# VectorE's list work in a four-layer graph network: list 0 spread over layer 0, one order chain in products 2 and 3, row gathers ahead of pair gathers

## The chip, the cores and the metric

The kernel runs on one core of a Trainium2 chip. The metric is the device time of one execution in microseconds (us), the median of several runs. The core has five engines that work from queues of their own: TensorE (PE in the profile, with its weight loads as PEld), VectorE (DVE), ScalarE (ACT), GpSimd (POOL) and SyncE (SP, which here only issues loads). They wait for each other through semaphores.

## What is computed

Four graph layers over the same 4096 x 4096 adjacency matrix `adj` (float32, about 1 entry in 500 not zero, a full diagonal), with `x` of 4096 x 128:

```python
x = _layernorm(x + _L0_gnn_ref(x, adj, adj, L0_gnn_W, L0_gnn_a))   # attention over positive entries
x = _layernorm(x + _L1_gnn_ref(x, adj, ...))                       # two Chebyshev convolutions, K = 3
x = _layernorm(x + _L2_gnn_ref(x, adj, ...))                       # attention with 4 heads
x = _layernorm(x + _L3_gnn_ref(x, adj, ...))                       # (adj @ h / deg) W_neigh + h W_self

# in layer 1
def cheb_conv(x, L, W, b):
    Tx0 = x
    out = Tx0 @ W[0]
    Tx1 = L @ x
    out = out + Tx1 @ W[1]
    for k in range(2, W.shape[0]):
        Tx2 = 2.0 * (L @ Tx1) - Tx0
        out = out + Tx2 @ W[k]
        Tx0, Tx1 = (Tx1, Tx2)
    return out + b
```

So layer 1 needs four products with `adj`: product 1 (`adj @ x`), product 2 (`adj @ t1`), product 3 and a fourth one (the code runs that one inside the function for the sparse layers).

## The kernel before

**Chunks and blocks.** `adj` is stored transposed and cut into 8 x 8 chunks of 512 x 512. A load brings one chunk of 1 MB as a tile [128, 4, 512]; five buffers (`ld`) take turns, and every load is issued on SP's queue. A block `ib` is a column of eight chunks. In products 1 to 3 one chunk means eight TensorE instructions of line 714 (4 matmuls in float32, each of two passes) into the block's sum `pacc`. `propagate` runs over blocks and chunks, and after each chunk it calls a hook `seen(ib, n, c, a)`. The hooks of a product are numbered through: h = 0 to 47 in product 2 (blocks 2 to 7, eight chunks each), h = 0 to 39 in product 3 (blocks 3 to 7). A dictionary `plan` says what is begun at which hook.

**Lists.** Since `adj` is sparse, the kernel also makes a list of the entries of each row. `take` finds, for each of the four rows of 128 in a chunk, the eight largest entries and their places (`max`, line 1359, and `max_index`, line 1360). A diagonal chunk is first copied by ScalarE, quarter by quarter, into the one buffer `copied` (line 1356), and VectorE takes the diagonal out (line 1358). `build(c)` turns what was found for group c of rows into a list, in three steps: step 1 sorts (and gives `count`, line 1386), then TensorE multiplies it (line 1410), step 2 makes `spread`, TensorE multiplies again (line 1434), and step 3 gives the indices that the gathers use. Groups 0, 1 and 2 (`PAIRED`) are finished early. List 0 is found in layer 0 by `first_list`, four rows in one go whenever a chunk with j = 0 comes by (lines 377 and 378).

**Gathers.** With lists 0 and 1 the blocks 0 and 1 of product 2 are left out of the dense product: their 8 units of 128 rows are summed from gathered rows. `pull(u)` issues nine indirect loads on GpSimd (line 1480), each followed by a small `pause` (line 1526); `weigh(u)` multiplies and adds the rows on VectorE (lines 1514 and 1517); `product(u)` gives them to TensorE (lines 1587 and 1589). In product 3 blocks 0, 1 and 2 are done so (12 units, lines 1645 to 1656), each `product(u)` calling `pull(u + 2)`; in the fourth product, blocks 0 and 1 again (lines 1989 and 1991). `fetch(c, n)` issues n of the 36 gathers of `pairs` for group c (the entries that a row has in both directions), and `paired(c)` puts them in place; a unit of group c can only be weighed behind that. `values(c)` issues 12 gathers of entries for group c.

**Block ends.** In product 2 VectorE makes `t2T` out of `pacc` (line 762), and `second_end` gives it to TensorE (lines 769 and 774) with ScalarE and VectorE between (lines 701 to 704). In product 3 ScalarE copies `pacc` (line 805), TensorE transposes, VectorE copies the result (line 807), and the rows are stored in a table in HBM from which later gathers read.

**Order.** Outside of the last layers the instructions of an engine are put in order by a planner, at build time, from costs and due times that it reckons with. `tc.keep_in_program_order` pins an instruction to the order of the program. In product 2 the takes, the adds of `weigh` (line 1517) and `paired` are pinned so, and on GpSimd every gather; steps of `build`, the block ends' `t2_of` and the copies of line 807 are the planner's to place.

**Layer 0** reads each chunk once, in two passes over rows i: VectorE makes a mask `pos` of the chunk (line 329), TensorE sums it (line 398), ScalarE counts bad entries (line 382), and TensorE multiplies the chunk (line 410). When a row of eight chunks is done, `scores(i)` copies the sums (`parts`, line 445), and TensorE goes on from there (line 405). `keep_busy` adds idle matmuls (line 341) in the first rows.

Of the kernel before, what the change touches and what calls it, by code (L numbers as in the profile page):

```python
# [11 lines left out]
F32 = mybir.dt.float32  # L12
# [34 lines left out]
def adj_resnorm_d4(ctx: ExitStack, tc: tile.TileContext, x_in, xT_in, adj, adjT, pairs, diag_in, w0g, w0gT, a0, w1a, b1a,  # L47
# [234 lines left out]
    def layer0(ld, ps_acc, ps_tr, ps_mm):  # L282
# [9 lines left out]
        with tc.tile_pool(name="l0", bufs=1) as l0, tc.tile_pool(name="l0w", bufs=2) as l0w, \  # L292
# [74 lines left out]

            def first_list(i, a):
                top, at = firsts
                for k in range(TB):  # L370
                    row = a[:, k, :]
                    if i == 0:
                        row = x[:, k * TB:(k + 1) * TB, :].rearrange("p t f -> p (t f)")
                        nc.scalar.copy(row, a[:, k, :])
                        d = row[:, k * P:(k + 1) * P]
                        nc.vector.scalar_tensor_tensor(d, ident, less_own[0][:, k:k + 1], d, op0=ALU.mult, op1=ALU.add)
                    nc.vector.max(top[:, k, i, :], row)
                    nc.vector.max_index(at[:, k, i, :], top[:, k, i, :], row)

# [79 lines left out]
            for i in range(2):  # L459
# [5 lines left out]
                for n, j in enumerate(order):  # L465
# [14 lines left out]
                    if j == 0:  # L480
                        first_list(i, a)
                    if n == 1 and rest:
                        diagonal_product(*rest)
                        diagonal_sums(*rest)
# [15 lines left out]
            def sums_of(i, j, pe, first, last, pool=ld, name="chunk"):  # L500
# [4 lines left out]
                if j == 0:  # L505
                    first_list(i, a)
                return j, a, pos
# [5 lines left out]
            for i in range(2, NB):  # L513
# [55 lines left out]
                if i == 5:  # L569
                    tc.keep_in_program_order(nc.sync.dma_start(x, x_in.rearrange("(t p) f -> p t f", p=P)))  # L570
# [91 lines left out]
    degrees, firsts, less_own = [], [], []  # L662

    def network(usual):

        with ExitStack() as whole:
# [3 lines left out]
            with ExitStack() as first, ExitStack() as l1h_pool:  # L670
                ps_acc, ps_tr, ps_mm = [first.enter_context(tc.tile_pool(name=n, bufs=2, space=PSUM, reuse_waits="tile"))
                                        for n in ("ps_acc", "ps_tr", "ps_mm")]
                if usual:
# [4 lines left out]
                    less_own[:] = [early.tile([P, NT], F32, name="less_own")]  # L678
                    nc.scalar.dma_start(own_entries, diag_in)
                    nc.vector.tensor_scalar_mul(less_own[0], own_entries, -1.0)  # L680
# [10 lines left out]
                l1w = l1h_pool.enter_context(tc.tile_pool(name="l1w", bufs=2, reuse_waits="tile"))  # L691
                l1h = l1h_pool.enter_context(tc.tile_pool(name="l1h", bufs=1, reuse_waits="tile"))
# [5 lines left out]
                def elu(dst, p, bias, less):  # L698
                    r = l1w.tile([P, IB], F32, name="elu_r", bufs=1)
# [61 lines left out]
                def t2_of(t2T, p, cols):  # L761
                    nc.vector.scalar_tensor_tensor(t2T, p, 2.0, xT[:, cols], op0=ALU.mult, op1=ALU.subtract)
# [20 lines left out]
                for ib, blk, p in propagate(lambda jt: t1[:, jt, :], seen=second, blocks=[b for b in range(NB) if not usual or b not in LAST]):  # L783
                    t2T = l1w.tile([P, IB], F32, name="t2T")
                    t2_of(t2T, p, blk)
# [17 lines left out]
                for ib, blk, p in propagate(lambda jt: v[:, jt, :], beside=times_w1, seen=third, blocks=[b for b in range(NB) if not usual or b not in PAIRED]):  # L803
# [3 lines left out]
                    nc.vector.tensor_copy(w[:, ib * TB:(ib + 1) * TB, :], q)  # L807
                    if usual:
                        lists.store(1, ib, w)
# [480 lines left out]

    class Lists:
# [3 lines left out]
        def __init__(self, whole, first, layer, own_entries):  # L1295
# [9 lines left out]
            self.diag = own_entries  # L1305
            self.source = keep.tile([P, NT, NEAR + QT], I32, name="source")
# [41 lines left out]

        def take(self, ib, c, a, pinned=False):
            pin = tc.keep_in_program_order if pinned else lambda r: r  # L1350
            for k in range(TB):
                t = c * TB + k
                row = a[:, k, :]
                if ib == c:
                    row = self.keep.tile([P, IB], F32, name="copied")
                    nc.scalar.copy(row, a[:, k, :])
                    d = row[:, k * P:(k + 1) * P]
                    pin(nc.vector.scalar_tensor_tensor(d, ident, less_own[0][:, t:t + 1], d, op0=ALU.mult, op1=ALU.add))
# [3 lines left out]
        def indices(self, out, key):  # L1362

            miss = self.work.tile([P, key.shape[1], key.shape[2]], F32, name=f"miss{key.shape[2]}", bufs=1)
            nc.vector.tensor_scalar(miss, key, 0.0, float(N + 1), op0=ALU.is_le, op1=ALU.mult)
            nc.vector.scalar_tensor_tensor(out, key, -1.0, miss, op0=ALU.add, op1=ALU.add)

        def build(self, c, pinned=False):
            pin = tc.keep_in_program_order if pinned else lambda r: r
            work = self.work  # L1370
# [11 lines left out]
            nc.vector.tensor_scalar(flat(there), flat(top), 0.0, None, op0=ALU.is_gt)  # L1382
            nc.vector.tensor_reduce(deg, rows(there), AX.X, ALU.add)
            nc.vector.tensor_reduce(self.bad[:, 2, c:c + 1], deg, AX.X, ALU.max)
            nc.vector.tensor_scalar(deg, deg, float(-NEAR), 0.0, op0=ALU.add, op1=ALU.max)
            nc.vector.tensor_copy(count, deg)
            nc.vector.tensor_copy(flat(key), flat(found_at))
            nc.vector.tensor_tensor(rows(key), rows(key), self.first.rearrange("p s r -> p (s r)")[:, None, :].to_broadcast([P, TB, NB * 8]), ALU.add)
            nc.vector.tensor_mul(flat(key), flat(key), flat(there))
            pairs = top.rearrange("p k s r -> p (k s) r")  # L1390
            nc.vector.tensor_reduce(self.bad[:, 0, c:c + 1], pairs[:, :, 7], AX.X, ALU.max)
            nc.vector.tensor_tensor(twice, pairs[:, :, 0:7], pairs[:, :, 1:8], ALU.is_equal)
            nc.vector.tensor_mul(twice, twice, pairs[:, :, 1:8])
            nc.vector.tensor_reduce(self.bad[:, 1, c:c + 1], twice, AX.XY, ALU.max)
            for k in range(TB):
                row, left = rows(key)[:, k], rows(there)[:, k]
                for n in range(0, MOST, 8):
                    nc.vector.max(best[:, k, n:n + 8], row if n == 0 else left)
                    if n + 8 < MOST:
                        nc.vector.match_replace(left, best[:, k, n:n + 8], row if n == 0 else left, -1.0)  # L1400
# [719 lines left out]
```

## Time and profile before

| | us |
|---|---|
| median of 3 runs | 1672.21 (1670.91 to 1673.08) |
| the profiled execution | 1672.15 |
| its span, first to last instruction | 1670.4 |
| layer 0 | about 0 to 351 |
| product 1 | about 351 to 577 |
| product 2 | 577 to 834 |
| product 3 | 834 to 1037 |
| fourth product | 1037 to 1235 |
| gathered layers 2 and 3 | 1235 to 1670 |

| engine | busy in the span | in product 2 | in product 3 |
|---|---|---|---|
| TensorE | 89% | 233 of 257 us | 186 of 203 us |
| VectorE | 66% | 194 us | 121 us |
| GpSimd | 50% | 176 us | 160 us |
| ScalarE | 22% | 44 us | 15 us |

The stages are cut where TensorE's instructions go from one line to the next. A row of the timeline gives the start, the duration, the engine, the line, the operation, out<-in by the program's names, the shapes and the count; in square brackets stands the idle time of the engine just before, and what ended it. Where several instructions of one kind follow each other they are one row.

### The profile page before, as it was taken

To read this page: it belongs to the slowest core of one execution; us is meant where nothing else is said; L and a number is where in the kernel's file an instruction comes from. 1 tells how busy PE (TensorE), PEld (TensorE's weight loads), DVE (VectorE), ACT (ScalarE), POOL (GpSimd) and SP (SyncE) were. 2 spreads that over 40 slices of the span, in tenths; PEclk is the share of its full clock that TensorE was granted. 3 is DMA by queue.
4 is the path that set the end of the run, shared out by engine and by line. 5 is a ranking of instruction groups with operands and counts; after the bars stand their busy time and mean duration, and the time that the engine had idled before them with its cause. 6 is when DMAs were issued, how large, how long until landed. Compare 5 with 4: busy or idle time off the path is not lost.

```text
span 1670.4 us, 16412 instructions
## 1 busy us (share of the span) xinstructions
PE 1480.9 (89%) x4744; PEld 719.1 (43%) x4744; DVE 1096.5 (66%) x3204; ACT 374.8 (22%) x690; POOL 835.3 (50%) x1322
## 2 busy tenths in 40 slices
PE   5799999999999999599979899999945788888886
PEld 3344344554444444244434444454423344444444
DVE  4887554788979696977669622255435766656676
ACT  5575450110000011112200000022223111122234
POOL 0000000000234048848768878888727888888851
PEclk9899999999999999799989899999976788889998
DMA  9776775578798977476568878988846667778773
GB/s 346 301 292 252 277 251 209 193 250 307 286 345 307 310 267 265 144 262 218 197 236 287 277 252 284 328 297 286 294 106 186 196 205 239 243 239 264 250 190 104
DMA packets 106972, 419.30 MB, mean 251 GB/s; under 512 B 21556, under 2 KB 44088, under 8 KB 67064
## 3 DMA queue, kind: packets, MB, share of 16 engines
q1 hardware_dynamic: 59984, 360.01, 60.4%
q0 software_dynamic: 22656, 36.17, 8.6%
q10 hardware_dynamic: 24232, 21.98, 4.4%
q8 instruction: 39, 0.64, 0.2%
q14 instruction: 61, 0.50, 0.1%
HBM read 404.39 MB, written 13.70 MB: 250 GB/s over the span
## 4 chain that ended last, share of the span: by engine, by line
PE 50%; DVE 20%; POOL 12%; DMA 9%; issue 6%; ACT 3%; SPq 1%; ACTq 0%; DVEq 0%; POOLq 0%
PE pacc L714 19%; PE pacc L410 11%; PE pp L2013 7%; POOL got L1783 5%; DMA got<-table,source 5%; DVE at L1360 3%; POOL got L1480 3%; DVE top L1359 2%; PE pp L1894 2%; POOL both_ways L1480 2%; DMA got<-rows,source 2%; POOL idle L1526 2%; DVE gw L1819 2%; DVE acc L1907 2%; DMA chunk<-in_adjT 1%
## 5 line engine op out<-in xcount | busy, mean ns | idle before, releaser
L1783 POOL DMA_INDIRECT got<-table,source x288 | 275.8, 958 | 88.3 <-issue 61.6
L1894 PE MATMUL pp<-chunk,xT 128*128 128x512 f32 x496 | 245.5, 637 | 1.0 <-ACT xT L1865 0.7
L714 PE MATMUL pacc<-chunk,x 128*128 128x512 f32 x512 | 222.6, 593 | 0.0
L1480 POOL DMA_INDIRECT got<-rows,source x180 | 181.4, 1008 | 56.6 <-issue 27.1
L410 PE MATMUL pacc<-chunk,hw 128*128 128x512 f32 x408 | 192.1, 616 | 0.2
L1328 POOL IOTA i<- 128x384 int32 (+3 forms) x4 | 0.9, 238 | 360.7 <-PE pden L398 345.0
L2013 PE MATMUL pp<-chunk,w 128*128 128x512 f32 x384 | 170.2, 592 | 0.0
L714 PE MATMUL pacc<-chunk,t 128*128 128x512 f32 x384 | 170.0, 593 | 0.0
L714 PEld LDWEIGHTS pacc<-chunk,x 128*128 128x128 f32 x512 | 96.0, 190 | 114.9 <-issue 114.9
L714 PE MATMUL pacc<-chunk,v 128*128 128x512 f32 x320 | 144.9, 604 | 0.0
L1480 POOL DMA_INDIRECT both_ways<-in_pairs,both_at x108 | 106.7, 988 | 72.7 <-DVE both_at L1462 55.5
L1359 DVE MAX8 top<-chunk 128x8 f32<-128x512 f32 x196 | 128.4, 677 | 17.6 <-DMA chunk<-in_adjT 17.6
L1894 PEld LDWEIGHTS pp<-chunk,xT 128*128 128x128 f32 x496 | 95.4, 205 | 91.6 <-issue 85.8
L1360 DVE FIND_INDEX8 at<-top,chunk 128x8 uint16<-128x512 f32 x196 | 133.0, 684 | 0.0
L410 PEld LDWEIGHTS pacc<-chunk,hw 128*128 128x128 f32 x408 | 76.6, 196 | 93.7 <-issue 90.1
L1526 POOL TENSOR_TENSOR idle<-idle 128x1 f32<-128x1 f32 x489 | 111.2, 227 | 8.5
L1517 DVE SCALAR_TENSOR_TENSOR here<-got,back,here 128x128 f32<-128x128 f32 x120 | 42.2, 351 | 100.9 <-DMA got<-rows,source 98.7
L714 PEld LDWEIGHTS pacc<-chunk,t 128*128 128x128 f32 x384 | 71.1, 190 | 81.0 <-issue 81.0
L329 DVE TENSOR_SCALAR pos<-chunk 128x2048 bf16<-128x2048 f32 x66 | 80.2, 1220 | 37.5 <-DMA chunk<-in_adjT 29.8
L382 ACT ACTIVATE junk<-chunk 128x2048 fp8e4<-128x2048 f32 x51 | 97.4, 1910 | 32.9 <-DMA chunk<-in_adjT 32.2
L2013 PEld LDWEIGHTS pp<-chunk,w 128*128 128x128 f32 x384 | 70.5, 190 | 76.5 <-issue 76.5
L714 PEld LDWEIGHTS pacc<-chunk,v 128*128 128x128 f32 x320 | 60.5, 194 | 78.2 <-issue 78.2
(381 smaller groups left out, 2021.1 us busy)
## 6 DMA issues: line engine op xcount, KB each, us to landing
chunk<-in_adjT SPq DMA_DIRECT2D x326, 1024.0 KB, 5.9
keep<-in_adjT SPq DMA_DIRECT2D x13, 1024.0 KB, 8.3
spread<-spread ACTq DMA_DIRECT2D x16, 384.0 KB, 3.5
got<-table,source POOLq DMA_INDIRECT x288
chunk<-in_adjT ACTq DMA_DIRECT2D x4, 1024.0 KB
got<-rows,source POOLq DMA_INDIRECT x180
table<-rows ACTq DMA_DIRECT2D x8, 264.0 KB, 6.7
xT<-in_xT ACTq DMA_DIRECT2D x8, 256.0 KB, 6.7
```

The lines of the kernel that those rows point to most:

```text
L329: r = nc.vector.tensor_scalar(pos, a, 0.0, None, op0=ALU.is_gt)
L382: nc.scalar.activation(junk, a, AF.Relu, scale=-1.0, accum_out=bad[:, n:n + 1], saturate=False)
L410: in_order(nc.tensor.matmul(p, hw[:, j * TB + k, :], a[:, k, :], start=first and k == 0, stop=last and k == TB - 1))
L714: nc.tensor.matmul(p, stationary(c * TB + k), a[:, k, :], start=n == 0 and k == 0, stop=n == NB - 1 and k == TB - 1)
L1359: pin(nc.vector.max(self.top[:, t, ib, :], row))
L1360: pin(nc.vector.max_index(self.at[:, t - TB, ib, :], self.top[:, t, ib, :], row))
L1480: tc.keep_in_program_order(nc.gpsimd.indirect_dma_start(out, None, of, bass.IndirectOffsetOnAxis(ap=index, axis=0)))
L1517: r = nc.vector.scalar_tensor_tensor(here, got[:, j, 0:F], self.back[:, u, j:j + 1], here, op0=ALU.mult, op1=ALU.add)
L1526: return nc.gpsimd.tensor_tensor(self.idle[:, 0:1], of, self.idle[:, 1:2], ALU.mult)
L1783: nc.gpsimd.indirect_dma_start(got[t][:, j, :], None, table, bass.IndirectOffsetOnAxis(ap=lists.source[:, t, j:j + 1], axis=0))
L1894: nc.tensor.matmul(p, y[:, t0 + k, :], a[:, ib % (TB // n), k, :], start=k == 0, stop=k == n - 1)
L2013: nc.tensor.matmul(p, w[:, c * TB + k, :], a[:, k, :], start=n == 0 and k == 0, stop=n == NB - 1 and k == TB - 1)
```

## The change

It has five parts.

1. **List 0 in layer 0.** `first_list` no longer works on the chunk: ScalarE copies the whole chunk into one half of the tile `x` (not in use yet), and the four row searches are put in a deque, one to be taken out after each of the following chunks. What is left is taken when the next chunk with j = 0 comes. The load of `x` moves from row i = 5 to row i = 7. The diagonal is set to zero with a comparison in place of an added negative, so the tile `less_own` goes, and the load of the diagonal moves from the program's start to the set-up of the lists.
2. **One chain in products 2 and 3.** `chained` gives each VectorE instruction of the takes, the list steps, `weigh` (now with the `hot` tiles, line 1514), `paired`, the block ends' `t2_of` and the copies of line 807 an order-only dependency on the one before it in the program. `product`'s own VectorE instructions and the block ends' line 704 are not in it.
3. **Order of chunks in product 2.** 0, 4, 1, 5, 2, 6, 3, 7 in place of 0 to 7. Only chunks with c of 4 or more have takes there.
4. **Hooks of product 2.** The rows of units 0 and 1 are pulled at hook 0, ahead of list 1's 36 pair gathers; list 2 is built from hook 14 on, in place of 8; the units are weighed at other hooks, units 0 and 1 early, and their space is used again for units 2 and 3.
5. **Product 3.** Three row buffers in place of two; no gathers of `values(3)` at hook 5, both `values` at hook 36; the units are weighed up to three hooks earlier.

The buffer `copied` moves to another pool, where it shares its place with `elu_r` of the block ends.

```diff
+            takes = deque()
+
             def first_list(i, a):
                 top, at = firsts
-                for k in range(TB):
-                    row = a[:, k, :]
+                rows = a
+                if i < NB - 1:
+                    while takes:
+                        takes.popleft()()
+                    rows = x[:, i % 2 * (NT // 2):(i % 2 + 1) * (NT // 2), :].rearrange("p (k t) f -> p k (t f)", k=TB)
+                    nc.scalar.copy(rows, a)
+
+                def take(k):
+                    row = rows[:, k, :]
                     if i == 0:
-                        row = x[:, k * TB:(k + 1) * TB, :].rearrange("p t f -> p (t f)")
-                        nc.scalar.copy(row, a[:, k, :])
                         d = row[:, k * P:(k + 1) * P]
-                        nc.vector.scalar_tensor_tensor(d, ident, less_own[0][:, k:k + 1], d, op0=ALU.mult, op1=ALU.add)
+                        nc.vector.scalar_tensor_tensor(d, ident, 0.0, d, op0=ALU.is_equal, op1=ALU.mult)
                     nc.vector.max(top[:, k, i, :], row)
                     nc.vector.max_index(at[:, k, i, :], top[:, k, i, :], row)
+
+                for k in range(TB):
+                    takes.append(lambda k=k: take(k))
+                if i == NB - 1:
+                    while takes:
+                        takes.popleft()()
...
                     if j == 0:
                         first_list(i, a)
+                    elif takes and i and n > 1:
+                        takes.popleft()()
...
-                if i == 5:
+                if i == 7:
                     tc.keep_in_program_order(nc.sync.dma_start(x, x_in.rearrange("(t p) f -> p t f", p=P)))
...
-                    less_own[:] = [early.tile([P, NT], F32, name="less_own")]
-                    nc.scalar.dma_start(own_entries, diag_in)
-                    nc.vector.tensor_scalar_mul(less_own[0], own_entries, -1.0)
...
-                for ib, blk, p in propagate(lambda jt: t1[:, jt, :], seen=second, blocks=[b for b in range(NB) if not usual or b not in LAST]):
+                for ib, blk, p in propagate(lambda jt: t1[:, jt, :], order=[0, 4, 1, 5, 2, 6, 3, 7], seen=second, blocks=[b for b in range(NB) if not usual or b not in LAST]):
                     t2T = l1w.tile([P, IB], F32, name="t2T")
-                    t2_of(t2T, p, blk)
+                    r = t2_of(t2T, p, blk)
+                    if usual:
+                        lists.chained(r)
...
-                    nc.vector.tensor_copy(w[:, ib * TB:(ib + 1) * TB, :], q)
+                    r = nc.vector.tensor_copy(w[:, ib * TB:(ib + 1) * TB, :], q)
                     if usual:
+                        lists.chained(r)
...
+        def chained(self, r):
+            if self.last is not None:
+                tc.add_manual_dep(r.ins, self.last.ins.name, mybir.DependencyInfo(
+                    mybir.DependencyClass.NoSync, mybir.DependencyReason.DATA), reason="chained")
+            self.last = r
+            return r
...
         def build(self, c, pinned=False):
             pin = tc.keep_in_program_order if pinned else lambda r: r
+            vector = in_order_engine(nc.vector, self.chained) if pinned else nc.vector
...
-        got = places[0:2] + places[2:4] * (units // 2 - 1)
+        got = places[0:2] * 2 + places[2:4] * 2
...
-        for c, h in ((1, 0), (2, 8)):
-            build = lists.build(c)
+        for c, h in ((1, 0), (2, 14)):
+            build = lists.build(c, True)
             for n in range(3):
                 at(h + 3 * n, next, build)
-        at(6, fetch, 1, TB * E)
-        at(11, pull, 0)
-        at(12, pull, 1)
-        at(17, fetch, 2, 9)
-        at(18, lists.paired, 0)
-        at(30, lists.paired, 1)
-        for u, h in enumerate((20, 24, 28, 32, 33, 37, 40, 41)):
+        at(0, pull, 0)
+        at(0, pull, 1)
+        at(7, fetch, 1, TB * E)
+        at(8, lists.paired, 0)
+        at(26, lists.paired, 1)
+        for u, h in enumerate((9, 11, 27, 30, 33, 35, 41, 44)):
             at(h, weigh, u)
             at(h + 1, product, u)
-        for u, h in ((2, 25), (3, 25), (4, 29), (5, 33), (6, 34), (7, 38)):
+        for u, h in ((2, 12), (3, 13), (4, 25), (5, 25), (6, 35), (7, 37)):
             at(h, pull, u)
-        at(40, fetch, 2, TB * E)
+        at(26, fetch, 2, 12)
+        at(45, fetch, 2, TB * E)
...
-                got[u] = pool.tile([P, E, F], F32, name="got3")
+                got[u] = pool.tile([P, E, F], F32, name="got3", bufs=3)
...
-        plan = {5: [lambda: deque(lists.values(3), 0)]}
-        for u, h in enumerate((7, 9, 15, 18, 20, 23, 25, 28, 31, 33, 36, 38)):
+        plan = {}
+        for u, h in enumerate((6, 9, 11, 14, 16, 19, 22, 24, 27, 30, 32, 35)):
...
-        plan[36].append(lambda: deque(lists.values(4), 0))
+        plan[36].append(lambda: (deque(lists.values(3), 0), deque(lists.values(4), 0)))
```

## The prediction, made before the changed kernel was run

> **What bounds the kernel now.** I read the table by stages first, since each stage has its own limit.
>
> ```profile
> core 0: us, PE busy (x) PEld busy (x) DVE busy (x) ACT busy (x) POOL busy (x), PEclk, DMA share, GB/s
> 354.00:577.00 223.00, 223.00 (x562) 100.07 (x562) 195.72 (x571) 13.59 (x24) 44.02 (x80) 1.00 0.85 307
> 577.00:834.00 257.00, 233.12 (x689) 111.53 (x688) 194.24 (x568) 43.78 (x76) 175.99 (x288) 0.97 0.67 228
> 834.00:1037.00 203.00, 186.35 (x594) 91.36 (x593) 120.56 (x516) 14.54 (x31) 160.14 (x252) 0.95 0.79 268
> 1037.00:1235.00 198.00, 189.34 (x582) 94.83 (x580) 84.56 (x291) 47.09 (x88) 146.94 (x267) 0.99 0.80 270
> ```
>
> Product 1 is TensorE without a gap. Product 2 leaves it 24 us, product 3 some 17 us, at a lower clock besides. The second view is what TensorE waits for in products 2 and 3 (total us, times, longest):
>
> ```profile
> PE pmm L769 <- DVE t2T L762: 19.8, 5, 16.6
> PE u L1410 <- DVE count L1386: 7.9, 1, 7.9
> PE u L1434 <- DVE spread L1419: 7.3, 4, 6.1
> ```
>
> Every one is VectorE being late. The third view, the timeline, says why, and what happens in layer 0:
>
> ```profile
> 21.64 0.18 DVE L680 TENSOR_SCALAR less_own<-diag 128x32 f32<-128x32 f32 x1 [3.52 <-DMA diag<-in_diag]
> 48.68 1.87 PE L405 MATMUL ptr<-sel,parts 128*128 128x3 f32 x8 [4.59 <-DVE parts L445]
> 191.31 0.40 PE L398 MATMUL pden<-pos,both 128*32 128x512 bf16 x4 [2.90 <-DVE pos L329]
> ...
> 666.61 0.35 DVE L1517 SCALAR_TENSOR_TENSOR here<-hT,back,here 128x128 f32<-128x128 f32 x1 [14.30 <-DMA hT<-rows,source]
> 697.56 0.67 DVE L762 SCALAR_TENSOR_TENSOR t2T<-pacc,xT 128x512 f32<-128x512 f32 x1
> 698.29 2.07 PE L769 MATMUL pmm<-t2T,W1A 128*128 128x512 f32 x2 [16.59 <-DVE t2T L762]
> ...
> 863.58 0.16 PE L1410 MATMUL u<-count,below 128*128 128x4 bf16 x1 [7.91 <-DVE count L1386]
> 863.60 6.44 PE L714 MATMUL pacc<-chunk,v 128*128 128x512 f32 x8
> 967.58 1.04 POOL L1480 DMA_INDIRECT got<-rows,source  x1 [7.08 <-PE ptr L1645]
> 1132.23 0.49 PE L1989 MATMUL pp<-ident,here 128*128 128x128 f32 x2 [1.31 <-DVE here L1517]
> ```
>
> VectorE stands 14.30 us at 652 to 666 before unit 0's rows, which GpSimd gathers only behind 36 pair gathers; the takes pile up behind it, and block 4's `t2T` comes 30 us later. At 863 step 1 of list 4 sat behind a `weigh` that waited for rows in the same way. The last row shows GpSimd's lateness reaching TensorE in the fourth product.
>
> **Layer 0.** Four effects.
> - `less_own` goes: VectorE's 3.52 us and TensorE's 3.46 us behind it. The chunks themselves still arrive until 33 us (DMA share 0.9 there), so between 0 and 3.4; I take 2.
> - List 0 of row 0 stood ahead of `parts`: searches 42.41 to 49.3, TensorE idle 4.59. They go to row 1, after its third chunk: 4 x (0.35 + 0.68 + 0.08 + 0.69) = 7.2 us in, against 3 of row 1's own 4 searches (3 x 1.44 = 4.3) that go on to row 2. Net 4.6 - 2.9 = 1.7 at worst, 4.6 at best; I take 3.
> - In rows 1 to 4 a burst of 5.8 us becomes single searches of 1.4 us. TensorE's gaps on `pos` and `xp` between 74 and 128 (0.71, 2.36, 0.62, 1.27, 1.15) are 6.1 us; I take 2.
> - The load of `x` moves. In the trace the load after it takes SP's queue 8.23 us to issue, and 2.90 + 0.74 us of TensorE's idle follow at 191. At row 7 (about 247 us) it stands ahead of the next chunks just so, but with a DMA share near 0.6 in place of 0.85, and it lands long before line 588 first needs it at 299. Between -4 and +3.6; I take 2.
>
> The whole-chunk ScalarE copy is not in the trace. Its nearest row is line 382's 1.91 us for the same shape (four copies of line 1356 would be 2.5): six more of some 2 us, on an engine with 72 of 120 us busy between 60 and 180. I cost it at nothing; what it hides behind is TensorE's work on the same chunk, and without that it would delay the bad-count behind it, not a sum. Layer 0: -9 us (0 to -13).
>
> **Product 2, gathers.** 27 gathers at 791.4 to 826.4 come 1.35 us apart: 12.1 us for nine. The last rows of t1 are stored at 579.4, and a store lands some 6 us later. So, on the old clock: units 0 and 1 at 586 to 610; 36 pairs to 659; units 2, 3 to 683; units 4, 5 to 707 (their place is free when block 4 ends, 681); 12 pairs to 723; units 6, 7 behind `product(4)` and `product(5)`, to 762; 24 pairs to 794; the stage then ends near 819. Hooks: chunks of 3.43 us, block ends of 6.9, products of 1.1. `weigh(0)` at hook 9 is at 618 (rows there at 599), `weigh(1)` at 626 (611), `weigh(2)` at 697, `weigh(6)` at 770 (750). None waits; the least margin, 15 us, takes the 14.30 us away.
>
> **Product 2, VectorE's queue.** A take is 4 x 1.39 = 5.6 us; a diagonal one 10.4, since the ScalarE copies into the single `copied` come 2.6 us apart. A list of groups 0 to 2 costs about 6.5, 3.7 and 2.4 us by step, a `weigh` 9 x 0.29 = 2.6. TensorE's work without a stall is 384 x 0.429 (line 714) + 96 x 0.43 (769) + 14.4 (774) + 9 (products) + 1.2 = 230.6 us. By block:
>
> | block | VectorE, chained and 704 | TensorE until `t2T` |
> |---|---|---|
> | 2 | 29.0 + 5 waiting for list 1's matmuls - 1 early start | 27.5 (+1.7 before it needs t2T) |
> | 3 | 22.3 + 5.2 + 6.5 + 2.6 = 36.6 | 36.6 |
> | 4 | 27.1 + 6.1 + 1.8 = 35.0 | 35.0 |
> | 5 | 27.1 + 5.2 + 2.6 = 34.9 | 36.6 |
> | 6, 7 | 35.7, 34.7 | 43.5 each (with units' block ends) |
>
> VectorE is 4 us late at block 2 and carries that until block 6. Chained, `t2_of` can't be moved ahead of the last take of its block any more, so I count this as lost: 4. The small waits that stay (0.36, 0.76, 0.51, 0.41, 1.24, 0.21 and the like) are 4 us. VectorE also waited for ScalarE's 703 (14.9 us in 7), its 1512 (8.8) and TensorE (9.3); it had room then and has less now (200 of 240 busy); 3 more. 230.6 + 11 = 242 against 256: **-14 us**. The chunk order costs TensorE nothing, a chunk is a chunk; what it gives is that one take of 5.6 us falls on two chunks (6.9), where four takes (22.3) fell on four (13.7). Line 807's place in the chain has cover: VectorE is 60% busy in product 3.
>
> The clock is where a rule speaks against this. In the trace the pair behind the 16.59 us gap took 2.07 us where 1.02 is usual, and the eight behind 7.91 took 6.44 for 3.6, so a long gap costs 2 to 3 us more; the 2.90 us one at 191 costs less. The Trainium skill (TensorE: Matmul & The Clock Gate, "What's actually happening") says that one idle window of about 3.4 us is enough to halve the clock. By it a 4 us lag at block 2 is dear, and four such lags would give 10 us back. By the rows before 786 to 790, TensorE does six matmuls of the next block first when `t2T` is late, so the gap breaks up. I go by the rows.
>
> **Product 3 and the fourth.** Hook 6's `weigh(0)` now stands behind lists 3 and 4, so nothing of theirs waits for rows. A far list costs 6.5 + 9.3 + 2.6 us. From VectorE's start some 3 us ahead of the stage, list 4's `count` is there at +23 (TensorE wants it at +21) and its `spread` at +32 (at +27): stalls near 7.5 us and one slow spell, where 7.91, 6.12 and two slow spells stood. Product 3 would fall from 203 to about 191. But GpSimd holds it: 132 gathers from 846.5 to 1044.8, then 72 for the fourth product to 1150.6, and `product(7)` there at 1157.0, with TensorE waiting 1.58, 1.31 and 0.33. The change has as many gathers; the third buffer takes 7.08 us of waiting away, and `values(3)` now stand ahead of the fourth product's rows. Product 3's start to that `product(7)` is 323.5 us; TensorE alone would be 297; GpSimd's way is 13 (last rows of v) + 304 - 7 + 6.4 = 316.5. **-7 us.**
>
> Here the second rule weighs. These 132 gathers come 1.45 us apart ((198.3 - 7.1)/132), at 900 to 920 even 1.8, against 1.35 while VectorE only took lists. The Trainium skill (SBUF — State Buffer, "Who interferes with whom") says that VectorE's copies and tensor_scalars in a two-port mode shut GpSimd out for their whole length. By it, list steps packed into one chain ahead of the gathers slow only those beside them: the same sum. If they were spread evenly, 1.35 all through would give 204 x 0.1 = 20 us. I keep 1.45.
>
> **Sum.** -9 - 14 - 7 = -30 on 1672.15 of the profiled execution, whose span is 1670.4; the median is 1672.21, so the same -30 goes to it: **1642 us**.
>
> **The rivals.**
> - *Layer 0 gives nothing, GpSimd all of product 3's gain back* (20%): the searches in layer 0 are not in the chain, so the planner may bunch them as before. For it: TensorE is 95% busy from 60 on. Then -14 and a little: 1657.
> - *VectorE's order fills better* (15%): no lag in product 2 (-25), layer 0 -11, gathers at 1.40: 1627.
> - *The chain makes VectorE the bound* (10%), on the other side: in product 2 each of six `t2T` stands behind a take and its waits. The 33 us that VectorE waited there, no longer filled, are 5.5 a block. If each block end is 8 us late with 2.3 us of slow clock, product 2 is 230.6 + 6 x 10.3 = 292, +36, less 16 elsewhere: 1692. It decides from 6 to 7 us a block on. Against: 194 of 257 us busy.
> - *It moves nothing* (3%): the planner already had this order, and the rows' wait only changes place: 1672.
>
> **How the numbers follow.** The forecast has 52%, its own range 1629 to 1655. 0.2% is 3.3 us, about what a measurement here can tell from no change. Faster: 52 + 20 + 15 = 87, one off for the sum's uncertainty, 0.86; same 0.04; slower 0.10. The range reaches to the first two rivals: 1622 to 1665.
>
> **What would show it.** Right: no wait over 2 us of line 1517 for `hT` rows; no gap over 5 us at line 769; first `parts` near 44 us; product 2 at 236 to 248 us; the fourth product's first gather behind 24 `values`. Wrong: line 769's waits adding up to over 20 us in several pieces; VectorE waiting at line 1358 or 1411 with takes behind; `x` landing late at line 588; or product 3 gaining 12 us that the fourth keeps.

## The result, and the profile after

The changed kernel takes 1651.86 us (median of 6 runs, 1645.91 to 1654.25) against 1672.62 beside it: a ratio of 0.9871, 95% interval 0.9852 to 0.9889. The forecast was 1642, with a range of 1622 to 1665. The profiled execution took 1653.07 us, with a span of 1651.2. By stage, from the first matmul of each stage to that of the next:

| stage | before, us | after, us | difference | forecast |
|---|---|---|---|---|
| layer 0 | 350.9 | 335.7 | -15.2 | -9 |
| product 1 | 226.3 | 226.3 | 0 | 0 |
| product 2 | 256.3 | 239.7 | -16.6 | -14 |
| product 3 | 203.1 | 198.8 | -4.3 | with the fourth: -7 |
| fourth product, to the gathered layers' first sum | 223.0 | 236.3 | +13.3 | |
| gathered layers | 410.8 | 414.4 | +3.6 | 0 |

The last row is within chance: in this run and nine of those below, with the same code and data there, it lies between 409.1 and 416.4. So the total is inside the range, and its parts are not where I had them: two stages gave 9 us more than forecast, and the pair behind them took 9.0 where it should have given 7. That the two errors are of opposite sign and cancel in part is luck.

The table by stages of the kernel after:

```profile
core 0: us, PE busy (x) PEld busy (x) DVE busy (x) ACT busy (x) POOL busy (x), PEclk, DMA share, GB/s
335.70:562.00 226.30, 226.30 (x580) 102.04 (x579) 198.26 (x571) 14.17 (x25) 44.06 (x80) 1.00 0.86 307
562.00:801.70 239.70, 231.91 (x684) 111.28 (x683) 197.20 (x518) 43.45 (x74) 173.29 (x288) 0.99 0.72 245
801.70:1000.50 198.80, 187.73 (x598) 89.49 (x596) 159.03 (x573) 15.77 (x31) 148.24 (x231) 1.00 0.79 268
1000.50:1236.80 236.30, 194.61 (x584) 97.41 (x583) 90.55 (x315) 52.40 (x98) 175.16 (x310) 0.91 0.76 250
```

Product 2 leaves TensorE 7.8 us idle in place of 23.9, product 3 11.1 in place of 16.7. The fourth product leaves it 41.7 (33.3 before; 24.8 us of each is one wait at the stage's end, for the gathered layers), and the clock there falls to 0.91. What TensorE waited for (total us, times, longest), after:

```profile
PE pmm L785 <- DVE t2T L778: 5.2, 4, 3.0
PE u L1448 <- DVE count L1317: 1.7, 2, 1.2
PE u L1472 <- DVE spread L1317: 2.9, 3, 1.4
PE pp L2026 <- DVE here L1556: 11.8, 4, 6.2
```

The first three rows answer to 19.8, 7.9 and 7.3 us before. The fourth is new in its size: 3.2 us before. The timeline of after, at the places that were shown of before:

```profile
19.28 2.55 PE L358 MATMUL pmm<-WA,xT 128*128 128x132 f32 x16 [0.18 <-PE pmm L358]
41.46 1.05 PE L418 MATMUL ptr<-sel,parts 128*128 128x3 f32 x8
...
636.10 0.67 DVE L778 SCALAR_TENSOR_TENSOR t2T<-pacc,xT 128x512 f32<-128x512 f32 x1
636.82 3.78 PE L785 MATMUL pmm<-t2T,W1A 128*128 128x512 f32 x4 [2.96 <-DVE t2T L778]
...
861.02 0.97 POOL L1518 DMA_INDIRECT got<-rows,source  x1 [3.29 <-PE pacc L730]
...
886.10 0.97 POOL L1518 DMA_INDIRECT got<-rows,source  x1 [12.53 <-issue]
...
1022.70 0.97 POOL L1518 DMA_INDIRECT got<-rows,source  x1 [0.15 <-issue]
1030.75 0.35 DVE L1556 SCALAR_TENSOR_TENSOR here<-got,back,here 128x128 f32<-128x128 f32 x1 [29.24 <-DMA got<-rows,source]
1037.91 0.77 PE L2026 MATMUL pp<-ident,here 128*128 128x128 f32 x2 [6.21 <-DVE here L1556]
```

TensorE no longer waits behind `less_own` (first row; 3.46 us before), nor at `parts` (second row). The longest wait for `t2T` is 2.96 us. But GpSimd stands still in product 3 for 3.29 us and then for 12.53 us (2.01 and 7.08 before), the second time with no releaser that the profile can name. The fourth product's first row gather comes at 1022.70, 22.2 us into the stage (before: 8.5), VectorE stands 29.24 us for it, and TensorE behind VectorE. To `product(7)` of the fourth product it is 332.3 us from the start of product 3, where it was 323.5 and the forecast said 316.5.

### The profile page after: what moved, and what is told of

It is laid out like the page before. It is cut to its first block, busy times and chain, and to the rows that moved or that the text cites. A ratio compares the mean times of both kernels' runs of the same rounds, so it can differ in the third digit from the quotient of the medians.

```text
span 1651.2 us, 16460 instructions
## 1 busy us (share of the span) xinstructions
PE 1478.5 (90%) x4744; PEld 714.2 (43%) x4744; DVE 1138.4 (69%) x3203; ACT 385.5 (23%) x693; POOL 833.1 (50%) x1322
## 4 chain that ended last, share of the span: by engine, by line
PE 46%; DVE 25%; POOL 14%; issue 6%; DMA 6%; ACT 3%; ACTq 0%; DVEq 0%; POOLq 0%
PE pacc L730 15%; PE pacc L423 12%; POOL got L1820 6%; PE pp L2050 5%; DMA got<-table,source 4%; PE pp L1931 3%; POOL got L1518 3%; DVE at L1397 3%; DVE top L1396 2%; POOL idle L1563 2%; DVE here L1556 1%; POOL value L1518 1%; DVE same L1317 1%; DVE gw L1856 1%; DVE acc L1944 1%
## 5 line engine op out<-in xcount | busy, mean ns | idle before, releaser
L423 PE MATMUL pacc<-chunk,hw 128*128 128x512 f32 x408 | 188.7, 607 | 0.8 <-DVE hw L466 0.7
L1863 PE MATMUL u<-gw,into 128*128 128x132 f32 x192 | 33.2, 317 | 68.3 <-DVE gw L1856 68.3
```

Source lines behind the costliest of these rows:

```text
L423: in_order(nc.tensor.matmul(p, hw[:, j * TB + k, :], a[:, k, :], start=first and k == 0, stop=last and k == TB - 1))
```

## Experiments on products 3 and 4: where the gain went

**The values behind the rows.** GpSimd's 24 value gathers of lists 3 and 4 go behind the fourth product's own rows.

```diff
-        plan[36].append(lambda: (deque(lists.values(3), 0), deque(lists.values(4), 0)))
...
-                for c in (5, 6, 7):
+                for c in (3, 4, 5, 6, 7):
                     yield from lists.values(c)
```

> After, with the 24 value gathers of lists 3 and 4 moved from product 3 to behind the fourth product's own rows, on GpSimd's queue. Theory A (GpSimd's order cost the fourth product its 13.3 us): its first row gather starts near 1008 us, as soon as the last rows of w are stored, and not at 1022.7; the four waits of line 2026's kind (11.8 us) fall under 3 us, the fourth product from 236.3 to 222 to 226 us, and the time to about 1640 (0.981 of before). Theory C (the fourth product is longer by its clock, 0.91, or by chance): the waits go but the stage stays at 232 to 238, and the ratio at 0.987. Theory B (the gathers' pitch of 1.44 to 1.59 us decides): stage near 230, ratio 0.984.

Measured: 1634.68 us, 0.9781 of before (0.9767 to 0.9796). Layer 0 to product 3 stay within 0.3 us of after; the fourth product is 223.7 us, 12.6 less. (The rest of the gain lies in the gathered layers, 410.8 us for 414.4, and is within chance.) The timeline and the waits of this kernel:

```profile
1006.11 0.97 POOL L1518 DMA_INDIRECT got<-rows,source  x1 [15.23 <-DMA rows<-w]
...
PE pp L2025 <- DVE here L1556: 2.8, 2, 1.5
```

GpSimd now waits 15.23 us for product 3's last rows of `w` to be stored, and begins 5.1 us into the fourth product. In that wait there was room for 11 gathers at 1.35 us; the change put 24 in. Theory A holds in place and size. The clock of 0.91 was a consequence, not a cause: it is 0.93 here, and TensorE's busy time in the stage is 4.5 us less beside 8.1 us less of idle time.

**The list steps spread.** Product 3's list steps come at every second chunk from the start, not at each of the first five.

```diff
-            if h < 5 or h % 2:
+            if h % 2:
                 next(build, None)
```

> After, with the steps of lists 3 to 7 in product 3 at every second chunk from the start, where the first five chunks have one each. Theory A (the 12.53 us that GpSimd stands idle for a buffer are VectorE's list steps ahead of weigh(1) in the chain): product(1) comes near 45 us into the stage in place of 81, the wait is under 2 us, and GpSimd ends its work of product 3 about 12 us earlier; the fourth product's rows then start near 1008, and the time falls by 8 to 14 us, to 0.980 to 0.982. Theory B (pitch): the wait goes, but the pitch beside spread list steps rises to 1.6 all along, and the sum stays within 3 us of after. Theory C: product 3 shortens by some us, the fourth product stays at 236.

Measured: 1638.90 us, 0.9807 (0.9785 to 0.9829). The same product, unit 1's, in the timeline of after and then of this kernel:

```profile
882.71 1.00 PE L1682 MATMUL ptr<-got,hot 128*128 128x128 f32 x6
```

```profile
863.60 1.00 PE L1682 MATMUL ptr<-got,hot 128*128 128x128 f32 x6 [1.59 <-DVE hot L1553]
```

With `product(1)` 62.5 us into the stage in place of 81.0, the 12.5 us wait is gone: GpSimd gathers from 815.6 to 962.0 without a wait over 0.6 us, and then waits 5.14 us before the last nine rows. The fourth product's rows start at 1012.6 and the stage is 225.6 us, 10.7 less. The forecast of 45 us for `product(1)` and of 1008 for the rows was too good, the direction and the sum were right. Theory B falls: the 99 gathers come 1.48 us apart. After has 1.60 for its first 36, or 1.51 without the wait of 3.29 us among them, and 1.45 for the next 72: 1.47 in all without waits. Product 3 itself stays at 198.7, with TensorE busy for 187.5 of it.

**Both.** The two edits together.

> Both edits at once. Theory A: they take away the same lateness of GpSimd, so they add up only in part: the fourth product near 222 and product 3 at 190 to 195, 1634 to 1640 us, 0.977 to 0.981. Theory B or C: no more than the better one alone, 0.984 to 0.987.

Measured: 1636.85 us, 0.9788 (0.9772 to 0.9803); product 3 198.0, the fourth 224.6. Product 3 did not shorten to the 190 to 195 that I expected. The two gains do not add up, because they take away the same lateness and behind it stands the store of `w`: with the lists spread, the place of the 24 values is worth 1.0 us (225.6 to 224.6), and not 12.6. The values alone have the lowest median of the versions that ran where before took 1670 to 1681 us, faster than both kernels; from the two together they can't be told apart.

**Two buffers.** Product 3's rows get two buffers again.

```diff
-                got[u] = pool.tile([P, E, F], F32, name="got3", bufs=3)
+                got[u] = pool.tile([P, E, F], F32, name="got3")
```

> After, with two buffers for product 3's rows in place of three. Theory A: unit 2's gathers wait for product(0) (56 us into the stage) and unit 3's for product(1) (81 us), so GpSimd stands idle some 12 us and then 12 us more, and the fourth product begins its rows 12 to 14 us later: 1662 to 1668 us, 0.994 to 0.997. If the buffers are not what counts (C): 0.987.

Measured: 1661.77 us, 0.9937 (0.9922 to 0.9952); product 3 is 213.2 us (+14.4), the fourth 233.0 (-3.3). GpSimd's timeline of this kernel:

```profile
861.06 0.97 POOL L1518 DMA_INDIRECT got<-rows,source  x1 [17.91 <-PE pacc L730]
886.12 0.97 POOL L1518 DMA_INDIRECT got<-rows,source  x1 [12.54 <-issue]
```

The first comes 3.4 us after the start of `product(0)`, the second 3.4 us after that of `product(1)`, as the 886.10 of after does. That names what the profile left as "issue": the buffer of unit 1. So the third buffer takes GpSimd's two waits from 30.5 us to 15.8 and is worth 9.9 us here, and the wait that it should end was moved from unit 3's gathers to unit 4's.

## Experiments on product 2: which part did it

**No chain.** The takes, `paired` and the sums of `weigh` keep the program's order as before; all else on VectorE is the planner's to place.

```diff
-        def chained(self, r):
+        def chained(self, r, keep=False):
+            return tc.keep_in_program_order(r) if keep else r
...
-            pin = self.chained if pinned else lambda r: r
+            pin = tc.keep_in_program_order if pinned else lambda r: r
             for k in range(TB):
...
-            pin = self.chained
+            pin = tc.keep_in_program_order
...
-                pin(nc.vector.scalar_tensor_tensor(here, got[:, j, 0:F], self.back[:, u, j:j + 1], here, op0=ALU.mult, op1=ALU.add))
+                r = nc.vector.scalar_tensor_tensor(here, got[:, j, 0:F], self.back[:, u, j:j + 1], here, op0=ALU.mult, op1=ALU.add)
+                if pinned:
+                    tc.keep_in_program_order(r)
```

> After without the order chain on VectorE: the takes, line 1540's copies and the sums of weigh keep the program's order, as before; the list steps, the one-hot rows, t2T and the copies of w are again the planner's to place. Theory R (the rows ahead of the pairs carry product 2's gain of 16.6 us; the chain only fixes an order): product 2 stays at 238 to 244 us, product 3 at 196 to 203. Theory Q (the chain carries it: without it t2T or the list steps fall behind takes and weigh again): product 2 back at 248 to 256 with over 10 us of waits of TensorE for t2T, and product 3's 6 to 8 us waits for count and spread return; ratio near 1.000.

Measured: 1661.69 us, 0.9914 (0.9890 to 0.9938). Product 2 is 267.5 us: 27.8 more than after and 11.2 more than before. The waits and the timeline of this kernel:

```profile
PE pmm L785 <- DVE t2T L778: 30.6, 3, 24.2
...
628.01 0.59 DVE L1554 TENSOR_SCALAR hT<-iota,into_column,back 128x128 f32<-128x128 f32 x2
652.87 0.35 DVE L1557 SCALAR_TENSOR_TENSOR here<-hT,back,here 128x128 f32<-128x128 f32 x1 [24.28 <-DMA hT<-rows,source]
653.14 0.68 DVE L778 SCALAR_TENSOR_TENSOR t2T<-pacc,xT 128x512 f32<-128x512 f32 x1
653.88 2.07 PE L785 MATMUL pmm<-t2T,W1A 128*128 128x512 f32 x2 [24.20 <-DVE t2T L778]
```

It is the stall of before again, in unit 2 in place of unit 0, with the rows ahead of the pairs: the planner puts unit 2's `weigh` ahead of list 2's second step, 24 us before its rows are there, and `t2T` behind it. That is theory Q; the prediction stood on the other. At the same time product 3 is 196.6 us and the fourth product 222.4, with GpSimd's 108 gathers of rows unbroken from 841.7 to 998.9 and `product(1)` 59.4 us into the stage (81.0 in after, 59.2 in before): in product 3 the chain is what puts `weigh(1)` behind the lists. One wait of 8.2 us for `count` came back there, as theory Q had it, and product 3 is shorter all the same.

**Pairs first.** Product 2's plan as before, but in the chain.

```diff
-        for c, h in ((1, 0), (2, 14)):
+        for c, h in ((1, 0), (2, 8)):
...
-        at(0, pull, 0)
-        at(0, pull, 1)
-        at(7, fetch, 1, TB * E)
+        at(6, fetch, 1, TB * E)
+        at(11, pull, 0)
+        at(12, pull, 1)
...
-        for u, h in enumerate((9, 11, 27, 30, 33, 35, 41, 44)):
+        for u, h in enumerate((20, 24, 28, 32, 33, 37, 40, 41)):
...
```

> After with product 2's plan as before (list 2 from hook 8, pairs of block 1 from hook 6, rows from hook 11, the weighing from hook 20, the row places of before), all in the chain. Theory R: weigh(0) stands again behind rows that come behind 36 pair gathers, and now the whole chain stands with it: a wait near 14 us on VectorE, t2T late by 16 us or more, product 2 at 254 to 270, ratio 0.997 to 1.006. Theory Q (the chain alone): 240 to 246, ratio under 0.992.

Measured: 1648.61 us, 0.9834 (0.9815 to 0.9854); product 2 is 238.3 us. The waits and VectorE's timeline of this kernel:

```profile
PE pmm L785 <- DVE t2T L778: 4.1, 3, 2.2
...
661.27 0.87 DVE L1553 TENSOR_SCALAR hT<-iota,into_column,back 128x128 f32<-128x128 f32 x3
662.07 1.11 DVE L1556 SCALAR_TENSOR_TENSOR here<-hT,back,here 128x128 f32<-128x128 f32 x3
```

No wait for rows, with the rows behind 36 pair gathers (640.8 to 665.5). In the chain `weigh(0)` stands behind list 2's steps and the takes of its hooks, and comes at 98.7 us into the stage; in before it began at 74.3 and stood until 89.5. I expected 254 to 270 and was wrong.

**Plain order.** The chunks of product 2 in the order 0 to 7.

```diff
-                for ib, blk, p in propagate(lambda jt: t1[:, jt, :], order=[0, 4, 1, 5, 2, 6, 3, 7], seen=second, blocks=[b for b in range(NB) if not usual or b not in LAST]):
+                for ib, blk, p in propagate(lambda jt: t1[:, jt, :], seen=second, blocks=[b for b in range(NB) if not usual or b not in LAST]):
```

> After with product 2's chunks in the order 0 to 7. By the prediction's count the four takes of a block (22.3 us of VectorE) then fall on its last four chunks (13.7 us of TensorE), so t2T stands in the chain behind a last take that is about 8 us late; TensorE waits at line 785 some 6 us in each of six blocks, product 2 comes to 270 to 285 us and the ratio to 1.005 to 1.015. If the chain recovers in the first four chunks and the waits overlap with the next block's six matmuls: 245 to 252 us, 0.991 to 0.995. If the order is worth nothing: 240 us, 0.987.

Measured: 1652.57 us, 0.9854 (0.9834 to 0.9874); product 2 is 242.4 us, 2.7 more than after. TensorE's timeline of after, and then of this kernel, behind block 2:

```profile
593.87 2.74 PE L730 MATMUL pacc<-chunk,t 128*128 128x512 f32 x6
596.80 1.99 PE L785 MATMUL pmm<-t2T,W1A 128*128 128x512 f32 x4 [0.20 <-DVE t2T L778]
```

```profile
593.03 12.18 PE L730 MATMUL pacc<-chunk,t 128*128 128x512 f32 x28
606.70 1.98 PE L785 MATMUL pmm<-t2T,W1A 128*128 128x512 f32 x4 [1.49 <-DVE t2T L778]
```

The matmuls on `t2T` come 10.7 us later in the stage (I had counted 8), but the planner puts 28 matmuls of the next block ahead of them in place of 6. I had held those six for fixed. So a late `t2T` costs little here while the next block's chunks are there and no `weigh` stands in front. The waits for `t2T` are 5.9 us in all (5.2 in after), and 3.5 us more go to two late chunks. The 2.7 us are no larger than chance: in eight profiles with after's code for product 2 the stage lies between 237.1 and 239.9 us.

**The chain alone.** Both of the last two edits undone, the chain kept.

> After with both of product 2's other edits undone: its plan of before (rows behind the pairs) and its chunk order 0 to 7, the chain kept. Theory Q (the chain alone takes product 2's time down): 238 to 244 us, as with either of the two undone alone (238.3 and 242.4), ratio 0.983 to 0.988. Theory R2 (rows ahead and chunk order stand in for one another; one of them is needed): t2T is late again with over 10 us of waits at line 785, product 2 at 250 to 258, ratio 0.993 to 0.999.

**The chain in product 2 only.** It ends behind product 2, with the values late.

```diff
         def chained(self, r):
+            if self.free:
+                return r
...
         got, made = {}, {}
+        lists.free = True
...
```

> After with the chain ended behind product 2 (in product 3 only the sums of weigh keep the program's order, as before), and the 24 value gathers behind the fourth product's rows. Theory A (in product 3 the chain puts weigh(1) behind the front-loaded list steps, so GpSimd waits for its buffer): no idle stretch of GpSimd over 3 us in product 3, product 2 at 238 to 241, product 3 at 196 to 199, the fourth product at 222 to 224, the time 1629 to 1635 us (0.975 to 0.979), at best 3 us better than v_late. If product 3 needs the chain: TensorE's waits of 6 to 8 us for count and spread return and product 3 is 203 or more, 1638 to 1642.

Measured: 1827.80 and 1784.16 us, 1.0026 (0.9998 to 1.0055) and 0.9718 (0.9672 to 0.9764) of a kernel before that took 1830.79 us on that chip, where it took 1669.76 to 1680.68 in all others. Layer 0 and product 1 are the same there (336.4 and 226.3 us with the chain alone); from product 2 on many waits have no releaser that the profile shows. The longest waits of TensorE, of the kernel with the chain alone:

```profile
PE u L1624 <- DVE here L1556: 24.3, 3, 12.5
PE ptr L790 <- issue: 21.5, 2, 15.9
PE pacc L730 <- issue: 20.0, 28, 1.5
...
PE pmm L785 <- DVE t2T L778: 4.8, 3, 2.1
```

The waits for `t2T` do not come back, which speaks for the chain alone; the time does not (product 2 at 321.1 us, with such waits all through, and VectorE late with a unit's sums). So it stays open whether the chain needs one of the two others, and whether a chain that ends behind product 2 is better than the values alone. That the second of these two kernels gains 2.8% there cannot be put to one edit.

## Experiments on layer 0

One run each; the reading is the stage. In ten profiles with after's code for layer 0 it lies between 334.8 and 336.7 us, so differences are good to about 1 us.

**The own entries at the head.** They are loaded and multiplied at the start again.

```diff
                     own_entries = early.tile([P, NT], F32, name="diag")
+                    less_own = early.tile([P, NT], F32, name="less_own")
+                    nc.scalar.dma_start(own_entries, diag_in)
+                    nc.vector.tensor_scalar_mul(less_own, own_entries, -1.0)
...
-            nc.scalar.dma_start(self.diag, diag_in)
```

> After with the own entries loaded and multiplied by -1 at the head of the program again (the product is not used). If the wait for that load was on TensorE's path: the first sum of row 0 (pden<-pos,both) starts at 30 to 31 us in place of 27.5, and layer 0 is 338 to 339 us for 335.7. If the chunks set the start: 27.5 and 335.7.

Measured: layer 0 340.3 us, +4.6; the first sum of row 0 at 31.2 us, +3.7 (it lies between 26.5 and 27.9 in the other kernels). So the wait was on the path whole.

**Row 0's searches at once.**

```diff
-                if i == NB - 1:
+                if i in (0, NB - 1):
                     while takes:
```

> After with the four searches of row 0's list made at once, ahead of row 0's scores, and not during row 1. Two sizes for the step that I put at 3 us: by the traces the first scores and the spell of slow clock behind them (granted clock 0.74 against 0.90) are worth 5.7 us, so the first scores come at 46 to 48 us and layer 0 at 340 to 342; by the prediction's own count of queued searches, 338 to 339.

Measured: layer 0 338.6 us, +2.9. TensorE's timeline of this kernel:

```profile
48.42 0.62 PE L411 MATMUL pden<-pos,both 128*32 128x512 bf16 x4 [5.87 <-DVE pos L329]
```

The planner put `parts` ahead of the searches on its own (first scores at 40.1 us), and the searches then stood ahead of row 1's masks. So this is the price of four searches at once, but not of the wait at `parts` that stood in before.

**The load of x behind row 5.** Row 6's copy for list 0 then goes over half of the loaded `x`, so that part of `x`, and what follows from it, has other values; layer 0's work is the same.

> After with the load of x behind row 5 again. By the scores of the rows, which come 9.4 us earlier than before at row 4 and 15.2 at row 5, its move is worth 5.8 us: layer 0 at 340 to 342 us with two gaps on the chunks near 178. By the prediction: 337 to 339. If the spreading of the searches gave those 5.8 us: 336.

Measured: layer 0 340.0 us, +4.3. The stretch from row 4's scores to row 5's, of this kernel and then of after:

```profile
150.90:187.20 36.30, 33.92 (x119) 14.22 (x117) 20.66 (x38) 20.79 (x23) 0.00 (x0) 0.95 0.78 290
```

```profile
150.90:182.80 31.90, 31.90 (x117) 13.49 (x116) 22.72 (x40) 19.90 (x23) 0.00 (x0) 1.00 0.73 264
```

The 4.4 us are one gap of 2.38 us on a late chunk's mask and 2.0 us more of busy time at a lower clock (0.95 for 1.00).

## Why the prediction was right, and where it was not

- **Layer 0, -9 against -15.2.** The steps were right in direction and three sizes were not. `less_own` and its wait: 2, measured 4.6; the chunks did arrive sooner than I allowed. Row 0's searches: 3, measured 2.9, at another place than in before, so that the agreement is partly luck. The load of `x`: 2, measured 4.3. The bursts of rows 1 to 4: 2; between the scores of row 1 and of row 4 the two traces differ by 0.6 (-8.9 to -9.5). The runs account for 11.8 of the 15.2; the rest stays open. One term my sum had nowhere: the clock. The stretch from the first sum of row 0 to its first product, of before and then of after:

```profile
30.70:56.70 26.00, 16.88 (x89) 7.65 (x89) 22.62 (x53) 14.09 (x17) 0.00 (x0) 0.74 0.75 283
```

```profile
27.50:44.60 17.10, 13.23 (x81) 5.83 (x80) 13.70 (x34) 9.07 (x9) 0.00 (x0) 0.90 1.00 399
```

  With 5.3 us less of idle time went 3.7 us less of busy time, at a clock of 0.90 for 0.74; 8 of the 89 matmuls, four of them idle ones of `keep_busy`, are no longer in that stretch, so not all of it is the clock.
- **Product 2, -14 against -16.6, by the wrong cause.** The step "None waits; the least margin, 15 us, takes the 14.30 us away" gave the gain to the rows going ahead of the pairs. It was the chain: without it the wait is 24.28 us with the rows ahead, with it there is none with the rows behind. My margin took each `weigh` at its hook; without the chain the planner puts it earlier (unit 2's at 66 us into the stage, where I had 120). That -14 came near is luck. Neither the chunk order (242.4 against 239.7) nor the plan (238.3) is worth more than the spread of the stage while the chain stands; without both, it stays open.
- **Products 3 and 4, -7 against +9.0: the step that failed.** "GpSimd's way" to `product(7)` was right as the bound, and mis-sized by 15.8 us (316.5 against 332.3). "The third buffer takes 7.08 us of waiting away" was the largest term: the wait is not gone but 12.53, since `weigh(1)` and so unit 1's buffer stand behind the list steps that the change puts ahead. I had named what waits for rows in that chain, and not what waits for `weigh`. The rest is a wait of 3.29 us for unit 0's buffer where my sum kept one of 2.01, a first gather 1.5 us later in the stage, and 1.0 us of pitch, less 0.5 at the end. That `values(3)` stand ahead of the fourth product's rows I listed and priced at nothing, as the same number of gathers. By the first experiment the place of the 24 values, those of list 4 with them, is 12.6 us; behind a GpSimd that is not late it is 1.0. (The units' hooks of product 3 moved by up to four, not three.)
- **Product 3 for TensorE, 191 against 198.8.** Its waits are 11.1 us, not 7.5, in pieces of at most 1.6; the rest is 187.7 us of work that I had put lower.
- **The pitch of 1.45 us** holds: on the same count, 132 gathers of rows and values less the waits, it is 1.44. Spread list steps gave 1.48 for rows, packed ones 1.47: the reading that they slow only the gathers beside them, with the same sum, holds. Whether VectorE's two-port modes are what slows them no run here shows.
- **The clock.** I went by two rows against the Trainium skill (TensorE: Matmul & The Clock Gate, "What's actually happening"), by which one idle window of about 3.4 us halves the clock. The runs bear out neither as a rule for the length of a gap. In after, the four matmuls behind the gap of 2.96 us took 3.78 us and the next four 3.09, with a granted clock of 0.62 from 636 to 645 us. In the kernel with the load of `x` behind row 5 the same eight, behind a gap of 3.06 us at the same place, took 1.98 and 1.88, with the clock at 1.00 from 641 to 650. And the gap of 2.38 us in layer 0 went with 2.0 us of slower work, where in the plain order eight matmuls behind a gap of 2.38 us took 3.70 (3.60 is usual). The rows of these two that cost nothing:

```profile
641.48 1.98 PE L785 MATMUL pmm<-t2T,W1A 128*128 128x512 f32 x4 [3.06 <-DVE t2T L778]
```

```profile
680.79 3.70 PE L730 MATMUL pacc<-chunk,t 128*128 128x512 f32 x8 [2.38 <-DMA chunk<-in_adjT]
```

  So a gap below the skill's figure can bring 2 to 3 us of slower work with it, or none, and its length alone does not tell which. What does is not shown here.
- **The rivals.** Half of the first came: GpSimd gave back all of product 3's gain, and 9.0 us more; layer 0's gain came in full. The one on the other side, the chain as VectorE's bound in product 2, did not come: 197.2 of 239.7 us are busy. It came in product 3, where VectorE is busy 49.2 of 53 us at 833 to 886 (31 to 84 us into the stage), and reached the time by way of GpSimd's buffer.

## What to carry to other kernels

When a hand-written order puts a block of work ahead of an instruction, list who waits for what that instruction frees: a buffer that it gives back can hold another engine's queue, and the loss shows a stage later. On a queue that bounds two stages, count what stands between the first moment at which the next stage's data are there and its first transfer; work that is needed late goes behind. And test a multi-part change by undoing one part at a time: here the part with the clearest story (rows ahead of pairs) showed no gain beside the one that looked like bookkeeping.

## What was not expected of the hardware

The same kernel took 1830.79 us on one chip and 1669.76 to 1680.68 on the others. The two traces from that chip show no slower instruction in layer 0 and product 1, and behind them TensorE idle in pieces of up to 16 us without a releaser. What causes it was not settled.

Gaps of the same length cost the clock differently: with 2.38 us of waiting went 2.0 us of slower work in one place and none in another, and 8.1 us of waiting in the fourth product went with 4.5 us more of busy time.
